# Self attention's last tile in two halves, a rebuilt end of a fixed convolution, and two mixtures that score their last tile apart: one change to a twelve-block network on one Trainium2 core

## The chip, the core and the metric

The kernel is one program on one core of a Trainium2 chip. The core has a matrix engine (TensorE; PE in the profile, with its weight loads as PEld), VectorE (DVE), ScalarE (ACT), GpSimd (POOL) and SyncE, which here only issues transfers (SP). Matrix products land in PSUM, which has eight banks of 128 partitions by 512 floats; everything else lies in SBUF or in the device's memory. The metric is the device time of one execution, in microseconds (us). Before the change the median of three runs is 3099.72 us (3099.47 to 3116.72).

## The reference

Sixteen sequences of 64 tokens with 256 channels, so 1024 tokens, go through four rounds of cross attention, a sequence mixer and a feed-forward block, each with a layer norm in front and added to the stream. Four of the twelve blocks matter here.

```python
x = x + L1_attn(_layernorm(x), ...)   # the fixed convolution
x = x + L1_ffn(_layernorm(x), ...)    # a mixture: 8 experts, 2 for each token
...
x = x + L3_attn(_layernorm(x), ...)   # self attention
x = x + L3_ffn(_layernorm(x), ...)    # a mixture with a capacity for each expert

# L1_attn
xz = rms_normed(x) @ in_proj_w.T + in_proj_b
x_ssm, gate = split(xz, 2)                       # 512 channels each
x_ssm = silu(conv_full(x_ssm, conv_w) + conv_b)  # 512 to 512 channels, 4 taps in time
ssm = conv_per_channel(x_ssm, K) + x_ssm * D     # K: 64 taps for each channel, fixed by weights
out = (ssm * silu(gate)) @ out_proj_w.T + out_proj_b      # and the block adds its own input

# L3_attn, 16 heads of 16 channels
scores = cov(q, k) + var(q) * var(k) / 16
out = (softmax(scores) @ v) @ Wo

# L1_ffn, L3_ffn
top_w, top_i = top_k(softmax(x @ gate_w), 2)
y = sum over the 2 chosen experts of  w * expert(x)
```

## The kernel before

The stream `X` stays in SBUF as eight tiles of 128 tokens (`NT` = 8). Products are in 32-bit floats, and each matmul of the program is two PE instructions in the profile; a transpose is one. A scheduler orders each engine's instructions at build time, by priority and its own estimate of when things are ready. Where the code says `set_order(True)`, instructions issued through `self.mm`, `self.tr` and the queues `dve`, `act` and `pool` keep the program's order on their engine.

**The fixed convolution** (`mamba_conv`, lines 1126 to 1260). The 512 channels are four groups `c` of 128; tokens go in two halves `n` of 512. `project(c, n)` (L1162) makes the input projection: groups 0 to 3 are the convolution's input, 4 to 7 become the gates `gs` through a Silu. `conv(c, n)` (L1183) is 16 matmuls of 512 columns, then a Silu into `xs[c]`. Groups 0, 1 and 2 then go through `taps` (L1196): VectorE adds 64 shifted products over the time steps, one instruction a tap. Group 3 goes through TensorE instead: `tokens` (L1212) transposes it, and `toeplitz(i, more)` (L1221) makes 32 channels by small matmuls against matrices read from the device's memory; between its pieces it puts the projections of the gates. `gated` multiplies the tap sums by the gates into `o`. All the order is written out: convolutions 0, 1, 2, 3, then tokens, four Toeplitz quarters, then the gating of all groups, and `out_proj` (L1262) does four matmuls for each tile (one for each group of `o`) and adds the tile to `X` (L1270). One PSUM pool, `mid`, has eight banks.

**The layer norm** (`layernorm`, L225) works on tiles 0 to 3, 4 to 6 and 7: VectorE takes means and variances, GpSimd the root (`rsqrt`), VectorE scales into `xn`. `norm_T` (L261) adds transposes of `xn` into `xnT`, by halves of four tiles.

**Self attention** (`attn3`, L1981) runs a pipeline over the eight tiles. For tile `i`: `scores` (32 matmuls for all 16 heads in two PSUM banks, then the row maximum and its subtraction on VectorE), `exps` on ScalarE, `probs_T` (transposes), `values` (matmuls against `v`, divided by the sum), `values_T`, `keep_T` and `output`, which adds to `X`. The steps of tile `i - 1` lie between those of tile `i`. The last round of the loop has only tile 7's values left.

**The mixtures** (`ffn1`, L2563, and `ffn3`, L2688) normalize and transpose, then `choose` (L2262) makes the eight gate logits of every token: 16 matmuls of 8 columns into one bank `pgate`, all after the last transpose. VectorE finds the two best experts. `slots` (L2344) gives each choice a place in its expert's list and inverts the lists by matmuls: `inb` marks the place within a group of 128 (VectorE, four pieces), `at` the group, and `val` holds three values to be moved (token row, weight, target row); `at` and `val` are made by GpSimd. The first inversion gives the rows that `take` gathers from the device's memory into `xg`; the other two (`pw`) give weights and targets. GpSimd also issues those gathers and the loads of expert weights (`up`, `down`). Then experts run, and `add_sent` (L2486) reads the two results of each token back (`yk`), GpSimd adds the two, and VectorE adds the sum to `X` (L2505), then a last product (L2509).

Of the kernel before, what the change touches and what calls it, by code (L numbers as in the profile page):

```python
# [8 lines left out]
F32 = mybir.dt.float32  # L9
# [69 lines left out]
class Net:  # L79
# [145 lines left out]
    def layernorm(self, dst, src, eps=1e-5, twice=None, then=None):  # L225

        nc = self.nc
        st = self.small.tile([P, NT, 6], F32, tag="st", name="st")
        mv = self.small.tile([P, NT, 2], F32, tag="mv", name="mv")
        rs = self.small.tile([P, NT], F32, tag="rstd", name="rstd")
        for lo, hi in ((0, 4), (4, 7), (7, 8)):
            for t in range(lo, hi):
                nc.vector.bn_stats(st[:, t, :], src[:, t, :])
                nc.vector.bn_aggr(mv[:, t, :], st[:, t, :])  # L238
            if twice is None:
                self.rsqrt(rs[:, lo:hi], mv[:, lo:hi, 1], 1.0, eps, hi - lo)  # L240
            else:
                self.rsqrt(rs[:, lo:hi], mv[:, lo:hi, 1], 1.0 + twice, eps * twice, hi - lo)
            for t in range(lo, hi):
                nc.vector.tensor_scalar(
                    dst[:, t, :], src[:, t, :], mv[:, t, 0:1], rs[:, t : t + 1], ALU.subtract, ALU.mult
                )
            if then is not None and hi % 4 == 0:
                then(hi // 4 - 1)
        return mv
# [876 lines left out]
    def mamba_conv(self):  # L1126
# [10 lines left out]
        with ExitStack() as es:  # L1137
            one = es.enter_context(tc.tile_pool(name=f"{L}one", bufs=1))
            two = es.enter_context(tc.tile_pool(name=f"{L}two", bufs=2))
            mid = es.enter_context(tc.tile_pool(name=f"{L}mid", bufs=8, space=PSUM))  # L1140
# [42 lines left out]
            def conv(c, n):  # L1183
                ps = mid.tile([P, 512], F32, tag="m", name="psc")
                for i in range(16):
                    ci, k = divmod(i, 4)
                    self.mm(
                        ps, wc[ci][:, k, c * P : (c + 1) * P], xp[:, ci, n * HB : (n + 1) * HB, k : k + TQ], i == 0, i == 15
                    )
                if n == 0:  # L1190
                    xs[c] = two.tile([P, B, TQ], F32, tag="xs", name="xs", bufs=4)
                act.activation(
                    xs[c][:, n * HB : (n + 1) * HB], ps.rearrange("p (b t) -> p b t", t=TQ), AF.Silu, bias=self.col(f"{L}_conv_b", c)
                )

# [25 lines left out]
            def toeplitz(i, more):  # L1221
# [5 lines left out]
                for d in range(TB):  # L1227
                    if d % (TB // 4) == 0:
                        next(more)
                    for r in (slice(0, 64), slice(64, 128)):  # L1230
                        self.mm(ps[r, d, :], T[r, d, :], xt[r, :, i * TB + d])
                act.copy(yt[:, :, i * TB : (i + 1) * TB], ps.rearrange("p d t -> p t d"))

# [7 lines left out]
            sums = [taps(0, 0, HB), taps(0, HB, B)]  # L1241
            for c in range(1, 4):
                for n in range(2):
                    conv(c, n)
                if c < 3:
                    sums.append(taps(c, 0, B))
            for g in range(2):
                tokens(g)
            for i in range(P // TB):
                toeplitz(i, (n for h in range(2) for n in project(4 + i, h)))  # L1250
            for x in sums:
                gated(*x)
            for g in range(2):
# [4 lines left out]
                dve.tensor_tensor(o[:, 3, cols], ps, gs[:, 3, cols], ALU.mult)  # L1258
            self.set_order(False)
            self.out_proj(o, wo, mid)  # L1260
# [720 lines left out]
    def attn3(self):  # L1981
# [11 lines left out]
        with ExitStack() as es:  # L1993
# [137 lines left out]

            project(0)
# [6 lines left out]
            for i in range(NT + 1):  # L2139
# [22 lines left out]
                if i + 2 < NT:  # L2162
                    keep(i + 2)
            self.set_order(False)
# [97 lines left out]
    def choose(self, wg, d_x, one, mid):  # L2262
# [13 lines left out]
        pg = mid.tile([P, 512], F32, tag="m", name="pgate")  # L2276

        nc.scalar.activation(best[:, 3, 0:1], self.xn[:, 0, 0:1], AF.Exp)

        def logits(g):  # L2280
            for t in range(4 * g, 4 * g + 4):
                for k in range(2):
# [6 lines left out]
                    )  # L2289

        for g in range(2):
            logits(g)
# [51 lines left out]
    def slots(self, place, oh, r, gate, comb, val, i, NG, one, big, mid, taken):  # L2344
# [7 lines left out]
        dve, act, pool = (  # L2352
            self.queue(n, e) for n, e in (("dve", nc.vector), ("act", nc.scalar), ("pool", nc.gpsimd))
# [11 lines left out]
        pool.tensor_tensor(at[:, :, :NG], at[:, :, :NG], at[:, :, 1:], ALU.subtract)  # L2365
        spot = self.spot.rearrange("p k t -> p (k t)")
        pool.tensor_tensor(val[:, 0, :, :NG], at[:, :, :NG], bc(spot, 2, NG), ALU.mult)
# [13 lines left out]
        for h in range(4):  # L2381
            js = slice(h * J // 4, (h + 1) * J // 4)
            dve.tensor_tensor(inb[:, js], bc(low[:, js], 2, P), bc(self.lane, 1, J // 4), ALU.is_equal)
        pi = mid.tile([P, 512], F32, tag="m", name="pi")
# [9 lines left out]
        pool.tensor_tensor(gate, gate, bc(r, 1, 2), ALU.mult)  # L2394
        pool.tensor_tensor(val[:, 1, :, :NG], at[:, :, :NG], bc(gate.rearrange("p k t -> p (k t)"), 2, NG), ALU.mult)
        pool.tensor_tensor(val[:, 2, :, :NG], at[:, :, :NG], bc(self.token, 2, NG), ALU.mult)
# [89 lines left out]
    def add_sent(self, d_y, sent, last, src, g, row, one, pool, mid):  # L2486
# [9 lines left out]
        for t in range(NT):  # L2496
# [4 lines left out]
            nc.gpsimd.tensor_tensor(yk[:, 0], yk[:, 0], yk[:, 1], ALU.add)  # L2501
            yks.append(yk)
        y = last()
        for t in range(NT):
            nc.vector.tensor_tensor(self.X[:, t, :], self.X[:, t, :], yks[t][:, 0], ALU.add)  # L2505
# [57 lines left out]
    def ffn1(self):  # L2563
# [6 lines left out]
        with ExitStack() as es:  # L2570
# [6 lines left out]
            self.norm_T(mid, "m")  # L2577
            p, oh, pq, seen, prod, gate = self.choose(wg, d_x, one, mid)
# [109 lines left out]
    def ffn3(self):  # L2688
# [4 lines left out]
        with ExitStack() as es:  # L2693
# [9 lines left out]
            self.norm_T(mid, "m")  # L2703
            p, oh, pq, _, prod, gate = self.choose(wg, d_x, one, mid)
# [170 lines left out]
```

## Time and profile before

The profiled execution took 3099.45 us, of which its span is 3097.8 us; 1.65 us lie around it. TensorE is busy for 94% of the span.

| engine | busy us | share of the span |
|---|---|---|
| PE | 2926.3 | 94% |
| DVE | 1962.2 | 63% |
| ACT | 1343.7 | 43% |
| POOL | 733.3 | 24% |

| stretch of the span (us) | what runs there |
|---|---|
| 1184 to 1368 | fixed convolution, its `out_proj` included |
| 1368 to 1378 | last transposes and logits of the first mixture |
| 1378 to 1407 | its choice and lists, up to the first expert |
| 1407 to 1601 | its experts and their sums |
| 2829 to 2934 | self attention |
| 2934 to 2943 | last transposes and logits of the second mixture |
| 2943 to 2966 | its choice and lists |
| 2966 to 3095 | its experts, sums and the results' adds |

A share of busy time over the whole span says little here: the change touches short stretches, and each is read by what ends last in it. In a timeline, columns are start, duration, engine, line, operation, output and inputs, shape and count; the square brackets give the idle time before and what ended it. In a table by windows, each engine's busy time in a stretch is followed by the clock that TensorE was granted (1.00 is full), the share of the transfer engines and their rate.

### The profile page before, as it was taken

Reading aid. Unit: us, or ns where it says so; the run is one execution under the profiler, and the core shown is the slowest. Engines: PE = TensorE matmul, PEld = TensorE weight load, DVE = VectorE, ACT = ScalarE, POOL = GpSimd, SP = SyncE. Lnnn points to the kernel's source line nnn. Section 1 sums busy time; section 2 is a strip of 40 time slices with the busy share of each in tenths; the row PEclk is TensorE's granted clock in tenths of the full one; section 3 lists DMA queues with packets and bytes.
Section 4 is the critical chain, followed back from the end, with each engine's and each line's share of the span. In section 5 each row is a group of like instructions: output and inputs, shape, how many; then the busy total and the mean of one; then the engine's idle time right before and its main releaser. Section 6 shows DMA issues by size and latency. Waiting matters only on the chain.

```text
span 3097.8 us, 65295 instructions
## 1 busy us (share of the span) xinstructions
PE 2926.3 (94%) x27452; PEld 1779.4 (57%) x27452; DVE 1962.2 (63%) x4058; ACT 1343.7 (43%) x3027; POOL 733.3 (24%) x817
## 2 busy tenths in 40 slices
PE   8999999899999999979989999998999899998888
PEld 4666666666455555458864555545655455455667
DVE  6888886523766665971137777768874676765521
ACT  3555554511554451013324444549851255554222
POOL 1000002400110001014420101026771355552132
PEclk9999999999999999979999999998998999999889
DMA  2000000013223323027752222101111111110143
GB/s 77 32 32 32 22 22 19 18 31 101 65 72 101 98 60 84 21 88 272 291 187 63 73 73 75 60 13 45 41 58 31 64 58 65 62 55 15 60 146 125
DMA packets 75820, 225.22 MB, mean 73 GB/s; under 512 B 17415, under 2 KB 30586, under 8 KB 68616
## 3 DMA queue, kind: packets, MB, share of 16 engines
q1 hardware_dynamic: 47536, 115.57, 12.1%
q0 software_dynamic: 21744, 99.34, 9.4%
q10 hardware_dynamic: 6248, 6.14, 0.7%
q8 instruction: 217, 3.56, 0.5%
q14 instruction: 75, 0.61, 0.1%
HBM read 210.09 MB, written 14.49 MB: 72 GB/s over the span
## 4 chain that ended last, share of the span: by engine, by line
PE 81%; DVE 12%; ACT 2%; POOL 2%; issue 2%; DMA 1%; SPq 0%; DVEq 0%; POOLq 0%; ACTq 0%
PE pss L205 15%; PE o L205 13%; PE pu L205 8%; PE pd L205 7%; PE psp L205 6%; PE pkv L205 5%; PE py L205 4%; PE pst L208 4%; PE po L205 2%; PE pb L208 2%; PE psq L205 2%; PE psy L205 1%; PE pg L205 1%; DVE nm L72 1%; PE ptk L208 1%
## 5 line engine op out<-in xcount | busy, mean ns | idle before, releaser
L205 PE MATMUL pss<-cT,qw 128*32 128x256 f32 x8192 | 368.3, 386 | 17.3 <-ACT pr L72 17.2
L72 DVE TENSOR_REDUCE nm<-pss 128x2 f32<-128x512 f32 (+1 forms) x384 | 309.4, 862 | 83.4 <-PE pss L205 83.4
L205 PE MATMUL o<-pT,cx 128*64 128x512 f32 (+3 forms) x1088 | 351.7, 576 | 0.0
L72 ACT ACTIVATE pr<-pss,nmm 128x256 f32<-128x256 f32 x512 | 234.8, 484 | 161.9 <-DVE nmm L72 161.9
L205 PEld LDWEIGHTS pss<-cT,qw 128*32 128x32 f32 x8192 | 203.6, 109 | 147.0 <-ACT pr L72 24.5
L222 POOL TENSOR_SCALAR rs<-mv 128x8 f32<-128x8 f32 (+3 forms) x50 | 9.7, 195 | 995.8 <-DVE mv L238 536.6
L205 PEld LDWEIGHTS o<-pT,cx 128*64 128x64 f32 (+1 forms) x1088 | 134.3, 163 | 188.4 <-issue 161.8
L72 ACT ACTIVATE pr<-pr,sm 128x256 f32<-128x256 f32 x256 | 109.1, 497 | 202.8 <-DVE sm L72 202.8
L205 PE MATMUL pkv<-wx,cT 128*128 128x512 f32 (+1 forms) x512 | 190.7, 625 | 0.6 <-issue 0.6
L72 DVE TENSOR_SCALAR pr<-pr,sm 128x256 f32<-128x256 f32 (+1 forms) x384 | 170.0, 485 | 6.6
L72 DVE TENSOR_TENSOR_SCAN h<-dA,pb 128x512 f32<-128x512 f32 x128 | 154.7, 1218 | 15.6 <-PE pb L208 9.3
L1512 POOL TENSOR_TENSOR h<-h,cb 128x1024 f32<-128x1024 f32 x64 | 151.5, 2369 | 53.2 <-DVE h L72 51.2
L205 PE MATMUL pd<-wd,hT 128*128 128x256 f32 x656 | 151.5, 382 | 2.6 <-DVE hT L2678 1.4
L72 DVE STREAM_TRANSPOSE pT<-pr 128x1024 f32<-128x1024 f32 x128 | 151.8, 1224 | 2.2
L2455 DVE TENSOR_SCALAR y<-pd,row 128x256 f32<-128x256 f32 x39 | 18.9, 484 | 207.5 <-PE pd L205 154.3
L72 ACT ACTIVATE pr<-pss,nm 128x1024 f32<-128x1024 f32 x128 | 142.7, 1115 | 11.2 <-DVE nm L72 8.6
L208 PE MATMUL pst<-ident,pr 128*128 128x128 f32 x1024 | 141.5, 281 | 5.8 <-DVE sm L72 1.9
L72 ACT COPY pT<-pst 128x512 f32<-128x512 f32 x128 | 75.0, 586 | 164.2 <-PE pst L208 164.2
L208 PEld LDWEIGHTS pst<-ident,pr 128*128 128x128 f32 x1024 | 110.5, 142 | 62.0 <-ACT pT L72 26.5
L205 PEld LDWEIGHTS pd<-wd,hT 128*128 128x128 f32 x656 | 122.0, 190 | 30.3 <-DVE hT L2678 6.2
L1686 POOL TENSOR_TENSOR rnk<-rnk,mhalf 128x8 f32<-128x8 f32 (+1 forms) x84 | 130.2, 1549 | 7.0
L205 PE MATMUL py<-h,ident 128*128 128x512 f32 x256 | 130.9, 597 | 0.0
(564 smaller groups left out, 5722.2 us busy)
## 6 DMA issues: line engine op xcount, KB each, us to landing
cT<-in_ctxT SPq DMA_DIRECT2D x32, 768.0 KB, 4.8
cx<-in_ctxP SPq DMA_DIRECT2D x32, 768.0 KB, 4.2
cT<-in_ctxT SPq DMA_DIRECT2D x32, 512.0 KB, 4.0
cT<-in_ctxT SPq DMA_DIRECT2D x64, 256.0 KB, 4.8
offb<-d_off SPq DMA_DIRECT2D x16, 576.0 KB, 3.8
cb<-d_C SPq DMA_DIRECT2D x16, 512.0 KB, 3.7
wu<-in_L_ffn_w POOLq DMA_DIRECT2D x8, 1024.0 KB
wd<-in_L_ffn_w POOLq DMA_DIRECT2D x8, 1024.0 KB
```

Of the source, the lines that this page charges most:

```text
L72: ins = getattr(self.engine, op)(*args, **kwargs)
L205: self.in_order(self.nc.tensor.matmul(out, lhsT=lhsT, rhs=rhs, start=start, stop=stop))
L208: self.in_order(self.nc.tensor.transpose(out, in_, self.ident))
L222: nc.gpsimd.tensor_scalar(t[:p, :n], in_, scale, eps, ALU.mult, ALU.add)
L1512: nc.gpsimd.tensor_tensor(hs[i], hs[i], cbs[hf, g], ALU.mult)
L1686: nc.gpsimd.tensor_tensor(r, r, self.mhalf[:, : n * H], ALU.pow)
L2455: nc.vector.tensor_scalar(y[:, i, :], po[:, i * D : (i + 1) * D], weight[:, g + i : g + i + 1], None, ALU.mult)
```

## The change

*Fixed convolution.* The PSUM banks are split: `mid` keeps four, and four (`held`) hold the out-projection's sums `pos` of all eight tiles, two to a bank. `conv` becomes a generator `convolved`, so that it can be cut into pieces of four matmuls. The order becomes: convolution 0, gates 4, convolutions 1 and 3, gates 5, tokens, then the first Toeplitz quarter with convolution 2 laid between its matmuls, and only then the taps of group 2. The other three quarters carry the projections of gates 7 and 6 and the out-projection's shares of groups 0 and 1. The shares of group 3, then 2, come at the end; `X` is added to in pairs of tiles.

*Self attention.* The loop ends one round and one tile earlier, and `last_tile(7)` does that tile by halves of heads.

*Mixtures.* `norm_T` goes; `choose` has `layernorm` call `normed` after each of its three groups of tiles, which transposes the group and makes its logits. `pgate` moves to the pool `big`. In `slots`, `at` and `val` go from GpSimd to VectorE. In `add_sent`, the odd tiles' two results are added to `X` by VectorE one after the other, with no sum by GpSimd.

```diff
-            mid = es.enter_context(tc.tile_pool(name=f"{L}mid", bufs=8, space=PSUM))
+            mid = es.enter_context(tc.tile_pool(name=f"{L}mid", bufs=4, space=PSUM))
+            held = es.enter_context(tc.tile_pool(name=f"{L}held", bufs=4, space=PSUM))
...
-            def toeplitz(i, more):
+            def toeplitz(i, more, every):
...
-                    if d % (TB // 4) == 0:
-                        next(more)
+                    if (i * TB + d) % every == 0:
+                        next(more, None)
...
+            def part(c, t):
+                first, last = t % 2 == 0 and c == 0, t % 2 == 1 and c == 2
+                self.mm(pos[t // 2][:, t % 2], o[:, c, t * P : (t + 1) * P], wo[:, c, :], first, last)
+
+            def rest():
+                for i in (7, 6):
+                    for h in range(2):
+                        yield from project(i, h)
+                for c in range(2):
+                    for t in range(0, NT, 2):
+                        part(c, t)
+                        part(c, t + 1)
+                        yield
...
             conv(0, 1)
-            sums = [taps(0, 0, HB), taps(0, HB, B)]
-            for c in range(1, 4):
+            projects(4, 0, 1)
+            for x in (taps(0, 0, HB), taps(0, HB, B)):
+                gated(*x)
+            for c in (1, 3):
                 for n in range(2):
                     conv(c, n)
-                if c < 3:
-                    sums.append(taps(c, 0, B))
+            projects(5, 0, 1)
+            gated(*taps(1, 0, B))
             for g in range(2):
                 tokens(g)
-            for i in range(P // TB):
-                toeplitz(i, (n for h in range(2) for n in project(4 + i, h)))
-            for x in sums:
-                gated(*x)
+            third = (n for h in range(2) for n in convolved(2, h))
+            toeplitz(0, third, 4)
+            for _ in third:
+                pass
+            third_sum = taps(2, 0, B)
+            more = rest()
+            for i in range(1, P // TB):
+                toeplitz(i, more, 6)
+            for _ in more:
+                pass
...
+            gated(*third_sum)
+            for c in (3, 2):
+                for t in range(NT):
+                    part(c, t)
+                    if c == 2 and t % 2:
+                        X = self.X[:, t - 1 : t + 1, :]
+                        nc.vector.tensor_tensor(X, X, pos[t // 2], ALU.add)
             self.set_order(False)
-            self.out_proj(o, wo, mid)
```

```diff
+            def last_tile(t):
...
+                halves = [slice(0, 4), slice(4, 8)]
+                for gs in halves:
+                    for g in range(gs.start, gs.stop):
+                        c, h = divmod(2 * g, 4)
+                        for b in range(2):
+                            for hh in range(2):
+                                r = slice(64 * hh, 64 * hh + 64)
+                                self.mm(ps[r, g, b, :], qb[:, c, b, h + hh, :], ka[:, c, b * TQ : (b + 1) * TQ])
+                    dve.tensor_reduce(mx[:, gs], ps[:, gs], AX.X, ALU.max)
+                    dve.tensor_tensor(pr[:, gs], ps[:, gs], bc(mx[:, gs], 3, TQ), ALU.subtract)
+                    act.activation(pr[:, gs], pr[:, gs], AF.Exp)
+                values(t - 1)
...
+                turned(0)
+                values_T(t - 1)
+                keep_T(t - 1)
+                turned(1)
+                for i in range(2):
...
+                            self.mm(o3[r, h - 8 * i, :], pT[r, h // 2, h % 2, :], v[r, h, :])
+                    dve.reciprocal(ri[:, hs], o3[:, :, HD])
+                    dve.tensor_tensor(on[:, hs], o3[:, :, :HD], bc(ri[:, hs], 2, HD), ALU.mult)
+                output(t - 1)
+                for i in range(2):
+                    pt = mid.tile([P, 512], F32, tag="m", name="pto")
+                    self.tr(pt[:, :P], on[:, 8 * i : 8 * i + 8].rearrange("p h d -> p (h d)"))
+                    (act.copy, dve.tensor_copy)[i](oT[:, i], pt[:, :P])
+                st[t]["oT"] = oT
+                output(t)
...
-            for i in range(NT + 1):
+            for i in range(NT - 1):
...
+            last_tile(NT - 1)
```

```diff
+        def normed(lo, hi):
+            if hi - lo == 1:
+                ps = mid.tile([P, 2, P], F32, tag="m", name="psT")
+                for c in range(2):
+                    nc.tensor.transpose(ps[:, c], self.xn[:, lo, c * P : (c + 1) * P], self.ident)
+                nc.vector.tensor_copy(self.xnT[:, :, lo * P : hi * P], ps)
...
+            for t in range(lo, hi):
                 for k in range(2):
                     nc.tensor.matmul(
                         pg[:, t * 8 : (t + 1) * 8],
...
+            if lo == 0:
+                nc.scalar.activation(best[:, 3, 0:1], self.xn[:, 0, 0:1], AF.Exp)
+
+        self.layernorm(self.xn, self.X, parts=normed)
...
-        pool.tensor_tensor(at[:, :, :NG], at[:, :, :NG], at[:, :, 1:], ALU.subtract)
-        pool.tensor_tensor(val[:, 0, :, :NG], at[:, :, :NG], bc(spot, 2, NG), ALU.mult)
...
             dve.tensor_tensor(inb[:, js], bc(low[:, js], 2, P), bc(self.lane, 1, J // 4), ALU.is_equal)
+            if h == 0:
+                dve.tensor_tensor(at[:, :, :NG], at[:, :, :NG], at[:, :, 1:], ALU.subtract)
+                dve.tensor_tensor(val[:, 0, :, :NG], at[:, :, :NG], bc(spot, 2, NG), ALU.mult)
...
-        pool.tensor_tensor(gate, gate, bc(r, 1, 2), ALU.mult)
-        pool.tensor_tensor(val[:, 1, :, :NG], at[:, :, :NG], bc(gate.rearrange("p k t -> p (k t)"), 2, NG), ALU.mult)
-        pool.tensor_tensor(val[:, 2, :, :NG], at[:, :, :NG], bc(self.token, 2, NG), ALU.mult)
+        dve.tensor_tensor(gate, gate, bc(r, 1, 2), ALU.mult)
+        dve.tensor_tensor(val[:, 1, :, :NG], at[:, :, :NG], bc(gate.rearrange("p k t -> p (k t)"), 2, NG), ALU.mult)
+        dve.tensor_tensor(val[:, 2, :, :NG], at[:, :, :NG], bc(self.token, 2, NG), ALU.mult)
...
-            nc.gpsimd.tensor_tensor(yk[:, 0], yk[:, 0], yk[:, 1], ALU.add)
+            if t % 2 == 0:
+                nc.gpsimd.tensor_tensor(yk[:, 0], yk[:, 0], yk[:, 1], ALU.add)
...
-            nc.vector.tensor_tensor(self.X[:, t, :], self.X[:, t, :], yks[t][:, 0], ALU.add)
+            for k in range(1 + t % 2):
+                nc.vector.tensor_tensor(self.X[:, t, :], self.X[:, t, :], yks[t][:, k], ALU.add)
```

## The prediction

> **What bounds the kernel now.** First the table by stage, since TensorE's 94% over the whole span hides stages with other limits. (Columns: busy time of PE, PEld, DVE, ACT, POOL, the clock granted, the transfers.)
>
> ```profile
> 1227.30:1309.60 82.30, 82.30 (x193) 35.88 (x193) 82.20 (x166) 4.13 (x6) 2.30 (x3) 1.00 0.05 12
> 1309.60:1347.20 37.60, 35.52 (x561) 22.51 (x559) 37.57 (x61) 8.74 (x15) 1.46 (x2) 0.99 0.11 32
> 1347.20:1378.30 31.10, 27.36 (x112) 23.73 (x112) 17.32 (x40) 2.66 (x4) 6.38 (x14) 0.72 0.36 117
> 1378.30:1406.90 28.60, 11.62 (x143) 8.79 (x143) 16.72 (x48) 2.29 (x4) 14.22 (x18) 0.54 0.68 263
> ```
>
> In the fixed convolution TensorE and VectorE are both full. Which ends last is in the chain of waits:
>
> ```profile
> 1260.86 0.66 DVE acc10e L72
> ...
> 1304.01 0.66 DVE acc20e L72
> ...
> 1347.16 0.61 DVE o L72
> 1347.82 10.10 PE po L205 x32
> ```
>
> It is VectorE: one group's taps take 1304.01 - 1260.86 = 43.15 us, they follow each other without a gap, and TensorE waits for the last. Then the timeline, for TensorE's pace and for what closes the other stages:
>
> ```profile
> 1213.39 96.35 PE L205 MATMUL psc<-xp,wc 128*128 128x512 f32 x224
> ...
> 1367.44 0.40 DVE L1270 TENSOR_TENSOR X<-X,po 128x256 f32<-128x256 f32 x1
> ...
> 1367.90 3.25 PE L268 MATMUL psT<-ident,xn 128*128 128x128 f32 x14 [3.08 <-DVE X L1270]
> ...
> 1371.86 6.41 PE L2283 MATMUL pgate<-wg,xnT 128*128 128x8 f32 x30
> ...
> 1405.97 0.41 PE L2439 MATMUL pxg<-ident,xg 128*128 128x128 f32 x2 [1.17 <-DMA xg<-L_ffnx,at]
> ...
> 2933.89 0.42 DVE L72 TENSOR_TENSOR X<-X,py 128x256 f32<-128x256 f32 x1 [2.17 <-PE py L205]
> ...
> 2959.96 4.08 PE L205 MATMUL pw<-inb,val 128*32 128x128 f32 x64 [2.96 <-POOL val L72]
> ```
>
> A mixture's transposes start when the last addition to X is done, though tiles 0 to 3 were normalized long before, and TensorE is then busy until the last logit. In the lists, the first mixture's first expert waits for gathered rows (a transfer), the second's later inversions for values that GpSimd makes.
>
> **Fixed convolution: a new wait.** An instruction pass of a 512-column matmul takes 96.35 / 224 = 0.430 us, so a half convolution is 32 x 0.430 = 13.76 us and a projection 1.72. From the end of convolution 0 (1213.39 + 13.76 = 1227.15) the new order on TensorE is: gates 4, 3.44; convolutions 1 and 3, 55.04; gates 5, 3.44; tokens, about 1.1 (to 1290.2); convolution 2's 27.52 with seven Toeplitz pieces before its last, each 0.52 and 0.20 of switching (a quarter in the timeline is 2.09 = 0.86 projection + 1.03 Toeplitz + 0.20). Convolution 2 ends at 1322.8 and its Silu (0.69, and 0.2 of hand-over) at 1323.7. In the old order it ended some 40 us earlier.
>
> VectorE meanwhile ends group 1's taps at 1260.86 + 1.2 (gating of group 0, moved ahead) + 43.15 = 1305.2 and its gating (1.14) at 1306.4, and its queue holds nothing else but group 2's taps. It idles 17.3 us. The last taps end at 1323.7 + 43.15 = 1366.9, **19.7 us later** than 1347.16. Queued behind them in VectorE's order: group 3's multiplication (0.65 a half), group 2's gating, the additions to X; TensorE waits with them. It runs out of Toeplitz work at 1290.2 + 33.3 + 29.3 + about 2 = 1354.8 (the three quarters: 12.4 Toeplitz, 6.9 projections, 6.9 for 16 early out-projection matmuls, 3.2 switching) and idles 13 us.
>
> What it buys: half of `out_proj` is done before. Let T be the end of the taps. Before, the last logit came at T + 31.1 (1378.27). After: the first late matmul runs at T + 0.8. TensorE restarted at 1347.8 after a wait of 1.9 us at clock 0.50 and had 1.00 only from about 1353.4. At 0.50 a 256-column matmul takes 0.85 us, then 0.43: in 5.6 us 6.6 of the 16, the rest 4.0, to T + 10.4. The Trainium skill ("TensorE: Matmul & The Clock Gate", Part 1: The HAM clock gate) has the clock back after one busy window of about 3.4 us; by that the matmuls would end 1.1 us sooner, and the whole 1.1 lower. VectorE, which took the statistics tile by tile in out_proj's shadow, now gets the pairs at T + 8 to T + 10.6, and owes four paired additions (0.68), eight statistics (0.62), eight scalings (0.36), two copies (1.1 together) and the last tile's root wait (1.3): 13 us, to T + 21. Last transposes, copy and four logit passes: 1.5; TensorE still has cold logits queued (0.2 a pass), about 1 more. I take T + 23.5; bounds T + 19 (the additions end at T + 11.3 and the second mixture's 8.3 us of transposes and logits follow at once) and T + 26 (nothing overlaps further). Gain 31.1 - 23.5 = 7.6. **Net +12.1** (+7.6 to +14.6). Four PSUM banks instead of eight: the third input projection may wait for the norm's last copies, 0.1; later turns of the four banks are 4 us or more apart with 0.7 us evictions, covered.
>
> **First mixture.** Scoring tile 7 apart is in the tail above; the table load for Exp (1.28) moves between ScalarE's two copies, hidden by queued logits, 1.3 if not. Lists: VectorE puts `at` and `val` (0.56 each by the 128x384 row) between pieces of `inb` (0.90 each), so the first inversion starts near 1390.9 instead of 1393.50, and rows come about 2 us earlier. But expert 0 waits for its gathered rows: `xg` was issued at 1397.96 and TensorE had it at 1405.97, behind five weight loads of 1 MB, running at 350 to 430 GB/s since 1390. Those start with `whose`, which is not moved. So -0.8 (less POOL work before loads 2 to 5). If the scheduler now fits a sixth load ahead of the rows, +2.7 (1 MB at 380 GB/s). I take +0.3, bounds -2.5 (one load less ahead) and +3.
>
> **Sums (both mixtures).** Four POOL additions fall (0.75 each); VectorE gets four more of 0.42, 20 in all, 8 us, about the time the reads take to land. The end stays VectorE's: -0.25 each, bounds -1 and +0.7. In the first mixture two of its eight additions of `yk` took 0.93 and 0.97, beside POOL's sums. A rule makes that speak against the change: the Trainium skill ("SBUF — State Buffer", Who interferes with whom) has a VectorE operation with two SBUF inputs and a GpSimd one that reads SBUF lock each other out. By it each of the four new additions could pay another 0.5: +2 a mixture instead.
>
> **Self attention.** From the scores' start (2916.41; unchanged until then) the old path is 17.9 us to the last addition's end, 2934.31. New: half the scores cold 1.84; maximum 0.65 and subtraction 0.65 for half 1 beside the second half's scores; half 2's end 2921.5, Exp 2922.2; tile 6's values on TensorE 2920.1 to 2922.1, transposes of half 1 to 2922.8, `values_T`, half 2's transposes to 2924.0, its copy 2924.8, value halves (1.0 each) to 2926.05, tile 6's output, two transposes and copies 2927.8, last output and addition 2929.5. **-4.8**; -3.3 if the clock falls on the way (the last four passes cold, +0.9, and transposes), -5.5 at best. The halved VectorE operations cost 0.1 more a pair (two of 0.67 against 1.23), in the count.
>
> **Second mixture.** Transposes and logits are TensorE's 7.82 busy of 8.40 us; apart or not, all 48 passes follow the last addition. Only the 0.5 gap goes: -0.4 (0 to -1.5 with a warm start). Its lists: `pw` ran at 2959.96, when GpSimd, between gathers, had made its values. On VectorE `at` and `val` (0.45 each) delay `inb` by 0.8, gate and the next two values end at 2957.0, then `pb` holds TensorE to 2957.8: `pw` 2.1 us earlier, with `xg` (issued about 0.8 later, 2.4 us to land) just there. -2.0 (-3 to +0.8, the last if the gather is late).
>
> Sum: 12.1 + 0.1 + 0.3 - 0.5 - 4.8 - 0.4 - 2.0 = **+4.8**. The profiled execution's 3099.45 gives 3104.25; the median of the runs shown is 0.27 above it, so 3104.5. Loads moved with these steps (gate weights' slots, the next block's weights on POOL) come free some us later and are used over 100 us on; cost nothing, or the 1 us issue if one lands in POOL's queue before a root.
>
> **Rivals.** (A) Not slower: the tail after the taps repays the wait. Place: from the last paired addition to the last logit. If VectorE keeps up, T + 19, 4.5 shorter: 3100.0; with the attention at its best 3099. It decides at T + 18.7. For it: warm, transposes cost 0.14 instead of 0.23. Against: 13 us of VectorE work behind pairs that come within 2.6 us. (B) The sixth load goes first in POOL's queue: +2.7 instead of +0.3, and the tail at T + 25: 3108.5. For it: two of POOL's operations that stood between the loads are gone. (C) The stall is not there, that is, group 2's convolution does not really come late: taps end at 1349.5, 17.3 less: 3087. Against: TensorE's order is written out, and the sum needs only rows.
>
> **How the numbers follow.** Forecast 0.50, A 0.20, B 0.22, C 0.04, other 0.04. So slower in any amount 0.74. Range 3095 to 3112: A with the good ends of lists, sums and attention (-5) below, B with the attention's and a list's bad ends (+3.5) above; that leaves out C, the rest and what lies beyond the bounds. A change of 1% (31 us), about what a measurement of this kernel can tell from none, no case reaches: 0.96 within, 0.01 faster, 0.03 slower, for a disturbance elsewhere in the schedule.
>
> **What would show it.** VectorE idle some 17 us before the third group's taps, ended by the Silu; TensorE idle 13 us before `part`, then at 0.50; last logit near 1390; `pxg` still waiting for `xg`; last attention addition 17.9 - 4.8 = 13.1 us after its scores start; `pw` waiting for no POOL row. No idle time before those taps would make the whole wrong; a tail under 19 us, its sign.

## The result, and the profile after

Over 17 runs of each kernel the median is 3115.54 us after the change (3110.28 to 3127.75) and 3108.94 us before (3099.44 to 3128.09). The ratio is 1.0008, with a 95% interval of 0.9992 to 1.0025: no change that can be told. (The two medians alone lie 6.6 us apart, which is within that interval.) As an absolute time the 3115.54 us lies above the forecast range of 3095 to 3112; but the kernel before, which the sum had started from at 3099.72, has moved up by 9.2 us as well, and the ratio applied to 3099.72 gives 3102.2. The two profiled executions are further apart, 3125.47 us (span 3123.8) after and 3099.45 before, because the one before is among the shortest of its kernel and the one after among the longest of its own. The 26.0 us between the two spans by stretch (worked out from the two traces):

| stretch | before | after | difference |
|---|---|---|---|
| start to the last addition ahead of the convolution | 1184.03 | 1180.37 | -3.7 |
| from there to the first use of the first mixture's logits | 194.28 | 210.90 | +16.6 |
| first mixture, to its last addition | 222.60 | 222.24 | -0.4 |
| unchanged code, to the scores of attention's last tile | 1315.51 | 1321.13 | +5.6 |
| last tile, to the last addition to X | 17.90 | 18.43 | +0.5 |
| from there to the first use of the second logits | 8.35 | 12.72 | +4.4 |
| rest | 155.09 | 157.99 | +2.9 |

Stretches of unchanged code move by -3.7 and +5.6, so a single profile can't price a change of this size. The table by windows of the changed kernel, with the windows at its own borders:

```profile
1226.10:1305.50 79.40, 79.40 (x249) 35.68 (x247) 79.19 (x163) 7.58 (x12) 0.00 (x0) 1.00 0.00 1
1305.50:1322.60 17.10, 17.10 (x114) 8.18 (x111) 0.06 (x2) 0.99 (x3) 2.76 (x4) 1.00 0.22 63
1322.60:1365.80 43.20, 30.59 (x434) 20.79 (x430) 43.17 (x66) 4.08 (x8) 0.99 (x2) 0.89 0.09 25
1365.80:1391.20 25.40, 19.20 (x80) 17.10 (x80) 12.54 (x35) 2.44 (x4) 6.34 (x14) 0.70 0.44 145
1391.20:1414.50 23.30, 12.55 (x136) 7.72 (x136) 17.16 (x50) 0.63 (x2) 10.18 (x12) 0.50 0.61 220
```

In the second line VectorE is busy for 0.06 of 17.10 us: the predicted stall. In the third TensorE has 30.59 us of work in 43.20, and nearly all of the rest is its 12.84 us wait for the last taps; the clock in the last two is low. The chain of waits of the changed kernel crosses the same places:

```profile
1318.19 3.65 PE psc L205 x8
1321.86 0.70 ACT xs L72
1322.58 0.79 DVE acc20e L72
...
1365.77 0.69 DVE o L72
1366.51 6.32 PE po L205 x20
1372.92 0.70 DVE X L1300
```

Before, it was VectorE from tap to tap without a break; now the end of convolution 2 sets the start of the last taps. The timeline of the changed kernel:

```profile
1202.04 5.37 PE L205 MATMUL psc<-xp,wc 128*128 128x512 f32 x8 [2.58 <-DMA wc<-in_L_attn_conv_wT]
...
1322.58 0.79 DVE L72 TENSOR_SCALAR acc20e<-xs,taps 128x1024 f32<-128x1024 f32 x1 [17.04 <-ACT xs L72]
...
1366.51 8.90 PE L205 MATMUL po<-wo,o 128*128 128x256 f32 x32 [12.84 <-DVE o L72]
...
1414.55 0.66 PE L2548 MATMUL pxg<-ident,xg 128*128 128x128 f32 x2 [0.51 <-DMA xg<-L_ffnx,at]
...
2938.14 1.15 PE L205 MATMUL pss<-ka,qb 128*64 128x64 f32 x32 [1.52 <-DVE pr L72]
...
2952.65 0.42 DVE L72 TENSOR_TENSOR X<-X,py 128x256 f32<-128x256 f32 x1 [1.38 <-PE py L205]
...
2952.99 2.68 DVE L244 TENSOR_SCALAR xn<-X,mv,rstd 128x256 f32<-128x256 f32 x3
...
2980.04 4.33 PE L205 MATMUL pw<-inb,val 128*32 128x128 f32 x61
```

The waits of 17.04 and 12.84 us are those that were forecast. `pxg` still waits for `xg` and `pw` for no row of GpSimd, as forecast too. Three lines were not forecast: the convolution waits 2.58 us for its fourth weight load; in attention the second half of the scores waits for VectorE's subtraction of the first half; three scalings of the norm behind attention take 2.68 us, where one takes 0.41.

### The profile page after: what moved, and what is told of

Its sections match the earlier page's. It is cut to its first block, busy times and chain, and to the rows that moved or that the text cites. A ratio compares the mean times of both kernels' runs of the same rounds, so it can differ in the third digit from the quotient of the medians.

```text
span 3123.8 us, 65282 instructions
## 1 busy us (share of the span) xinstructions
PE 2943.9 (94%) x27452; PEld 1787.5 (57%) x27452; DVE 1965.6 (63%) x4078; ACT 1343.8 (43%) x3029; POOL 721.2 (23%) x799
## 4 chain that ended last, share of the span: by engine, by line
PE 85%; DVE 9%; ACT 2%; DMA 1%; POOL 1%; issue 1%; SPq 0%; DVEq 0%; POOLq 0%; ACTq 0%
PE pss L205 15%; PE o L205 13%; PE pu L205 8%; PE pd L205 7%; PE psp L205 6%; PE pkv L205 5%; PE py L205 4%; PE pst L208 4%; PE psc L205 3%; PE po L205 2%; PE pb L208 2%; PE psq L205 2%; PE psy L205 1%; PE pg L205 1%; PE ptp L208 1%
## 5 line engine op out<-in xcount | busy, mean ns | idle before, releaser
L208 PEld LDWEIGHTS pst<-ident,pr 128*128 128x128 f32 x1024 | 109.8, 141 | 61.5 <-ACT pT L72 26.5
L205 PEld LDWEIGHTS pkv<-wx,cT 128*128 128x128 f32 (+1 forms) x512 | 64.3, 188 | 118.6 <-issue 92.2
```

Source lines behind the costliest of these rows:

```text
L205: self.in_order(self.nc.tensor.matmul(out, lhsT=lhsT, rhs=rhs, start=start, stop=stop))
L208: self.in_order(self.nc.tensor.transpose(out, in_, self.ident))
```

## The experiments

Twelve kernels ran. Stretches are named as in the table above; "T" is the end of the third group's taps, as in the prediction.

**One part at a time.** Three kernels take the kernel before and only the change's edits to `mamba_conv`, to `attn3`, or to the mixtures.

> The kernel before with the fixed convolution's new end alone; attention and mixtures as before. My theory: convolution 2 comes too late, so VectorE idles about 17 us ahead of the third group's taps, the taps end 18 to 20 us later than in the kernel before, and the shorter tail behind them returns 5 to 8 us: the stage from the last addition before it to the first use of the logits is 11 to 17 us longer, the run 11 to 17 us (0.35 to 0.55%) above the kernel before. Rival (clock): most of the 26 us between the two profiles is where cold stretches of TensorE's clock happened to fall; then the wait is there but the run lies within 5 us of the kernel before, and the stage is not over 8 us longer.

Measured: the stretch took 211.27 us, 17.0 more, with the stall (17.03 us), and T + 22.8 to the first use of the logits. Yet the median was 3107.95 us against 3113.05, ratio 0.9989 (0.9971 to 1.0006). So the profile went as my theory said and the time as the rival's. The profiled execution (3116.4) was one of the two longest of the twelve. A stretch that is 17 us longer with a run that is not suggests that the old end, in most executions, costs more than the first profile shows; the experiments below look for that.

> The kernel before with the halves of heads in self attention's last tile alone. My theory: the second half's scores wait 1.5 us for VectorE's subtraction of the first half, since both halves are one PSUM tile, and what the halves should have hidden is lost: 17 to 19 us from the start of the tile's scores to the last addition (17.9 before), and the run within 3 us of the kernel before. Rival (clock): the 18.4 us of the changed kernel came from a cold clock, and here it is 13 to 15.5 us, the run 2 to 5 us lower.

Measured: 20.0 us, worse than either theory, and 12.16 us instead of 8.35 from there to the logits, with code there that is unchanged; the clock was 0.50 for 58 us on end. The 1.52 us wait for VectorE is there as in the changed kernel. Median 3118.61, ratio 1.0019 (0.9998 to 1.0040): a loss of 6 us at the middle of the interval, though zero lies just within it.

> The kernel before with the mixtures' changes alone (last tile scored apart, values by VectorE, half of the sums by VectorE). My theory: in the second mixture VectorE's copies stand ahead of the last tile's statistics, so the stretch from the last addition to the first use of the logits is 10 to 12 us instead of 8.35; the first mixture's stretch from there to its first gathered rows at TensorE is 3 to 4.5 us shorter (27.7 before), but its experts take it back; in all the run is within 4 us of the kernel before. Rival (clock): the 12.7 us in the changed kernel is the cold clock alone, here 8 to 9 us, and the run is 3 to 6 us lower than the kernel before.

Measured: 10.27 us; first gathered rows at 23.02 us instead of 27.66; ratio 0.9991 (0.9966 to 1.0015). The time is the one forecast, but not its cause: VectorE did the last tile's statistics at once here. This profile holds the convolution of the kernel before, and shows what that first profile didn't. The timeline in the Toeplitz quarters, two lines of the kernel before first, then this one's:

```profile
1317.17 1.13 PE L205 MATMUL psi<-xnT,w_in 128*128 128x512 f32 x2
1318.22 1.10 PE L205 MATMUL psT<-xt,T 64*64 64x8 f32 x32
...
1346.94 2.07 PE L205 MATMUL psi<-xnT,w_in 128*128 128x512 f32 x2
...
1348.95 1.88 PE L205 MATMUL psT<-xt,T 64*64 64x8 f32 x32
...
1364.50 14.53 PE L205 MATMUL po<-wo,o 128*128 128x256 f32 x64
```

The clock had fallen at 1324.7 for 41 us. A projection of two passes took 2.07 us instead of 1.13, a piece of 32 small products 1.88 instead of 1.10; the quarters took 49.4 us instead of 32.4 and ended 14 us behind T, and the last addition of the out-projection came 34.0 us after T instead of 20.7.

**The late convolution undone.**

```diff
-            for c in (1, 3):
+            for c in (1, 2, 3):
...
-            third = (n for h in range(2) for n in convolved(2, h))
-            toeplitz(0, third, 4)
...
-            for i in range(1, P // TB):
-                toeplitz(i, more, 6)
+            for i in range(P // TB):
+                toeplitz(i, more, 8)
```

> As the kernel with the convolution's new end alone, but convolution 2 back between 1 and 3, all four Toeplitz quarters carrying the gates 7 and 6 and the early products. My theory: VectorE does not wait for the third taps (under 1 us), they end within 4 us of the kernel before's, TensorE ends its Toeplitz work at about the same time, the tail is about 25 us as in the changed kernel, and the run is 14 to 20 us lower than with the new end alone and 2 to 7 us lower than the kernel before. Rival (PSUM banks and order: the new end is slow for its four banks and its paired additions, not for the late convolution): the run is within 5 us of the kernel with the new end alone.

Measured: ratio 0.9989 (0.9967 to 1.0012). It tested nothing, because VectorE now waited 12.1 us for group 1's gates, whose projection had come to stand behind three convolutions. Mended by putting `projects(5, 0, 1)` behind convolution 1:

> The convolution's new end alone, with convolutions in the order 0, 1, 2, 3 and the gates 5 between 1 and 2, so that VectorE finds both the third group's input and group 1's gates ready; Toeplitz quarters with a dense piece after every 8 channels, as in the kernel before. My theory now has two parts: (a) the late convolution costs VectorE 15 to 19 us; (b) the small Toeplitz products let TensorE's clock fall in part of the executions, and the old end (a dense piece every 8 channels) pays some 12 us for it there. By it: no wait ahead of the third taps (under 1 us), they end at 1347 to 1353, 16 to 20 us sooner than in the kernel with the new end alone when the stage starts alike; the runs spread over 15 us or more, as the kernel before's do, the fastest below 3094, the median 3098 to 3106. Rival (the wait is free, since the tail takes it back): median within 3 us of the new end alone, 3105 to 3111.

Measured: no wait ahead of the third taps, T 140.7 us after the first tap (157.7 with the late convolution). Still the median was 3111.88, ratio 1.0008 (0.9985 to 1.0032), the runs from 3095.47 to 3121.72. In its profile the clock fell at 1345.4, in the middle of the quarters, without a wait:

```profile
1343.12 1.13 PE L205 MATMUL po<-wo,o 128*128 128x256 f32 x4
1344.18 1.10 PE L205 MATMUL psT<-xt,T 64*64 64x8 f32 x32
1345.22 1.95 PE L205 MATMUL po<-wo,o 128*128 128x256 f32 x4
1347.10 1.88 PE L205 MATMUL psT<-xt,T 64*64 64x8 f32 x32
```

The taps end 17.0 us sooner after the first tap than with the new end alone, and the first use of the logits comes at T + 35.4 instead of T + 22.8. So 17 us less stall bought nothing that the runs can tell: part (a) holds in the trace, and in this profile 12.6 us of it go where part (b) says.

**More dense pieces between the small products.** The gates 4 and 5 go into the quarters too.

```diff
-                for i in (7, 6):
+                for i in (4, 5, 7, 6):
...
             for i in range(P // TB):
-                toeplitz(i, more, 8)
+                toeplitz(i, more, 5)
+                if i == 1:
+                    for x in sums:
+                        gated(*x)
+                    third_sum = next(third)
```

> As the kernel named last, but the gates 4 and 5 also lie within the Toeplitz quarters, with a dense piece after every 5 channels (24 pieces instead of 16), and VectorE multiplies by the gates in the middle of the third taps. By part (b) of my theory the clock stays at 1.00 through the Toeplitz quarters in nearly all executions: the runs spread over 12 us or less, mean clock 0.962 or more, median 3092 to 3101 and at least 3 us below the kernel with a piece every 8 channels. Rival (the density of the pieces has nothing to do with the clock): same spread and median within 2 us of that kernel, or slower by the 2 us of switching more.

Measured: median 3102.05, runs from 3097.94 to 3106.32, mean clocks 0.963 to 0.967, ratio 0.9980 (0.9962 to 0.9999). The spread is a third of the other's, and all is as forecast but the median, 1 us above its range. The table by windows of this kernel, first the quarters, then the end:

```profile
1317.20:1354.00 36.80, 36.80 (x476) 22.66 (x477) 36.73 (x60) 6.61 (x11) 0.70 (x1) 1.00 0.08 25
1354.00:1382.90 28.90, 22.94 (x168) 19.20 (x166) 12.41 (x34) 2.92 (x5) 5.99 (x14) 0.81 0.39 128
```

Up to T TensorE is busy throughout at a clock of 1.00. Over all profiles: with a piece every 8 channels the clock fell in the midst of the quarters in 5 of 7, with one every 6 or 5 in none of 6, though in the four with one every 5 it came down within 0.7 us of the quarters' last product.

**No pieces at all.** The kernel before, gates first, then the quarters alone:

```diff
             for i in range(P // TB):
-                toeplitz(i, (n for h in range(2) for n in project(4 + i, h)))
+                projects(4 + i, 0, 1)
+            for i in range(P // TB):
+                toeplitz(i, iter(range(4)))
```

> The kernel before, the same work, but the gates' projections all ahead of the Toeplitz quarters, so that nothing dense lies between their small products. My theory (the small products let TensorE's clock fall, the dense pieces between them decide how often): it falls in nearly all executions; in the profile the clock is 0.50 over most of the last two quarters and the first use of the logits comes 38 us or more after the third taps' end (31.1 and 28.9 in the warm profiles of the old end, 41.3 in the cold one); no run under 3105, median 3113 to 3124. Rival (it is only the phase of the clock's windows, whatever lies between): spread, fastest runs (near 3096) and median as the kernel before's, within 3 us.

Measured: median 3101.47, ratio 0.9965 (0.9947 to 0.9984). My theory was right on the clock of the profile and wrong on its price. The table by windows, gates, quarters, end:

```profile
1317.80:1331.60 13.80, 13.80 (x34) 5.89 (x32) 13.80 (x15) 5.39 (x8) 0.00 (x0) 1.00 0.15 38
1331.60:1357.10 25.50, 25.50 (x513) 25.38 (x512) 25.46 (x48) 1.80 (x4) 0.70 (x1) 0.55 0.08 23
1357.10:1387.40 30.30, 26.16 (x121) 23.70 (x120) 14.46 (x37) 3.03 (x5) 6.24 (x14) 0.78 0.36 117
```

The quarters ran at 0.55, as predicted, but the 13.80 us of projections ran ahead of them at 1.00, and T + 33.5 is all it comes to. In the kernel before, a fall also halves the speed of every projection that lies between the quarters' products. An estimate from these rows: the small products alone would take 16 pieces of 1.03 us (from start to start, in the kernel before), 16.5 us, at full clock and took 25.5, so about 9 of the 17 us that the quarters lost in the profile above are theirs, and the other 8 the dense work's among them.

**Two PSUM tiles in attention.**

```diff
-                ps = ps_s.tile([P, 8, 2, TQ], F32, tag="s", name="pss")
+                pss = [pool.tile([P, 4, 2, TQ], F32, tag=tag, name="pss") for pool, tag in ((ps_s, "s"), (mid, "m"))]
...
-                for gs in halves:
+                for ps, gs in zip(pss, halves):
```

> Attention's last tile by halves alone, with the two halves' scores in two PSUM tiles instead of one. My theory: TensorE no longer waits 1.5 us for VectorE's subtraction between the halves; from the tile's first score to the last addition 15.5 to 18 us (20.0 with one tile), the run 2 to 6 us below the kernel with one tile and within 3 us of the kernel before. Rival (the wait is not what costs, the clock after the halves' small pieces is): the wait is gone, but the stretch is still 18.5 us or more, and the stretch behind it, to the logits, still 11 to 13 us.

Measured: 12.49 us, less than forecast; the wait is gone. From there to the logits 12.59 instead of 8.35, so 25.1 together, against 26.3 before: of 5.4 us saved, 4.2 went in the next stretch. Ratio 1.0011 (0.9990 to 1.0033); the profiled execution is the shortest of the ten. The timeline:

```profile
2912.10 3.68 PE L205 MATMUL pss<-ka,qb 128*64 128x64 f32 x64
...
2925.01 1.98 DVE L244 TENSOR_SCALAR xn<-X,mv,rstd 128x256 f32<-128x256 f32 x3 [0.43 <-POOL rstd L223]
...
2927.51 0.41 DVE L237 BATCH_NORM_STATS2 st<-X 128x6 f32<-128x256 f32 x1
...
2930.24 0.69 PE L268 MATMUL psT<-ident,xn 128*128 128x128 f32 x2 [2.21 <-DVE xn L244]
```

The last tile's statistics come 2.9 us after its addition (2924.16 + 0.42), behind scalings and a copy of other tiles.

**The last tile's statistics ahead.** In the mixtures alone, tiles 4 to 6 are handed to `normed` only when the last tile is scaled:

```diff
-            if parts is not None:
-                parts(lo, hi)
+            if parts is not None and hi != 7:
+                if hi == 8:
+                    parts(4, 7)
+                parts(lo, hi)
```

> The mixtures' changes alone, but tiles 4 to 6 are transposed and scored only after the last tile is scaled, so that VectorE does the last tile's statistics ahead of the copies of the others. My theory: in the second mixture the stretch from the last addition to the first use of the logits is 8 to 9.3 us (10.3 with the mixtures' changes as they are, 8.35 in the kernel before). Rival (TensorE's clock and order set it, not VectorE's order): 10 us or more.

Measured, in one execution: 10.32 us; my theory fell. What this profile shares with that of the mixtures alone is GpSimd's queue: a weight load (`wd`, 0.95 us to issue) stands between the two steps of the last root, which ends 3.6 us after the statistics instead of 2.6, and the logits behind it run at a clock of 0.50. That this makes up the difference is argued from the rows; no run took the load away.

**Put together.** Three kernels carry the dense pieces and the mixtures' changes, with the last products by pairs of tiles. The first keeps attention as before:

```diff
-            for c in (3, 2):
-                for t in range(NT):
+            for p in range(NT // 2):
+                for c, t in ((2, 2 * p), (2, 2 * p + 1), (3, 2 * p), (3, 2 * p + 1)):
                     part(c, t)
```

> The kernel with a dense piece every 5 channels, plus the mixtures' changes, attention as before; the last products go by pairs of tiles (group 2, then 3), and the last tile's statistics stand ahead of the copies. My theory: the savings add, since they lie in different stages: median 3094 to 3101, ratio 0.995 to 0.998, clock 0.963 or more. Rival (what a stage saves is lost in the next, as the first mixture's lists did with 4.6 us): within 2 us of the kernel with the dense pieces alone, or above it.

Measured: median 3101.68, ratio 0.9974 (0.9955 to 0.9994). By the median it is the rival, 0.4 us below the kernel with the dense pieces; the ratio lies in the theory's range too. The mixtures' changes add nothing that can be told. The second also has the two PSUM tiles, and VectorE's order held to the last statistics first:

```diff
-                nc.vector.bn_stats(st[:, t, :], src[:, t, :])
-                nc.vector.bn_aggr(mv[:, t, :], st[:, t, :])
+                dve.bn_stats(st[:, t, :], src[:, t, :])
+                dve.bn_aggr(mv[:, t, :], st[:, t, :])
...
+            if parts is not None and hi == 7:
+                roots(7, 8)
```

> As the kernel named last, but with attention's last tile by halves in two PSUM tiles, and VectorE held to the last tile's statistics ahead of the scaling of tiles 4 to 6. My theory: the halves save 5 us up to the last addition, and with the statistics first the norm behind does not give them back: from the last tile's scores to the first use of the logits 19 to 23 us (26.3 in the kernel before, 25.1 with two PSUM tiles alone), the run 2 to 6 us below the kernel named last. Rival (the clock that falls in the halves' small pieces takes it): 24 us or more, the run within 2 us of the kernel named last.

Measured: median 3102.87, ratio 0.9978 (0.9958 to 0.9997); 24.1 us from the scores to the logits. The rival's number, but not for its reason: the clock was 1.00 through the halves, which took 10.84 us, and fell only at 2938.1, behind them. Its timeline:

```profile
2935.97 0.30 POOL L2605 MEMSET zero<- 128x256 f32 x1
...
2936.21 2.55 DVE L72 TENSOR_SCALAR xn<-X,mv,rstd 128x256 f32<-128x256 f32 x1
...
2937.70 0.73 POOL L2462 MEMSET val<- 128x768 f32 x1
...
2938.69 0.19 POOL L222 TENSOR_SCALAR rs<-mv 128x1 f32<-128x1 f32 x1
```

One scaling took 2.55 us, as long as GpSimd wrote its constants, and the last root stood behind these. The third moves these constants behind the root:

```diff
         self.layernorm(self.xn, self.X, parts=normed)
+        const = constants()
...
+    def after_root(self, ins):
+        order = mybir.DependencyInfo(mybir.DependencyClass.NoSync, mybir.DependencyReason.DATA)
+        self.tc.add_manual_dep(ins.ins, self.last_root.ins.name, order, reason="after the norm")
```

> As the kernel named last (halves in two PSUM tiles, statistics first), but GpSimd's constants of the two mixtures stand behind the last tile's root in its queue. My theory: in that kernel VectorE's first scaling behind attention took 2.55 us instead of 0.41, because GpSimd was writing these constants from SBUF's side at the same time, and the last root stood behind them; with the constants behind the root all scalings take 0.32 to 0.55 us, and from the last addition to the first use of the logits it is 8.5 to 11 us (13.3 there); from the last tile's scores to there 19.5 to 22.5 us (24.1 there, 26.3 in the kernel before); the run 1 to 4 us below it. Rival (that scaling was long for another reason, and the cold clock sets the logits' time): a scaling of over 1 us is still there, or the stretch is 12 us or more; the run within 1.5 us of it.

Measured: 9.87 us to the logits, 22.4 in all, scalings of 0.40 to 0.81 us; median 3098.47 against 3112.35, ratio 0.9961 (0.9944 to 0.9978).

```profile
2930.73 0.96 POOL L186 DMA_DIRECT2D wd<-in_L_ffn_w  x1
2930.96 0.81 DVE L72 TENSOR_SCALAR xn<-X,mv,rstd 128x256 f32<-128x256 f32 x1
2931.77 0.18 POOL L226 TENSOR_SCALAR rs<-mv 128x1 f32<-128x1 f32 x1
```

In the trace the theory holds, but for one scaling of 0.81 us beside the issue of a load by GpSimd. Of the run, the stretch explains 1.8 us; the medians differ by 4.4, but the two were measured apart, and the intervals of their ratios to the kernel before overlap. This kernel has the lowest median of all, 0.2 to 0.6% below the kernel before.

## Why the prediction was right, and where it was not

The class was right, and so was the stall, the larger part of the largest term. The sum of +4.8 us lies in the interval of the runs (-2.5 to +7.8, from the ratio), but by luck: two of its terms, what the old end costs and what attention saves, are wrong by more than the sum.

- *The stall.* 17.3 us forecast, 17.04 measured; the taps end 19.7 us later by the forecast, 157.68 - 138.01 = 19.67 from the first tap; TensorE's wait 13 against 12.84. A written-out order and a row's duration are enough for this.
- *The tail*, T + 23.5 forecast, T + 25.4 and T + 22.8 measured: mis-sized by 2 at most, within its bounds. The late products restarted at 1366.51 and had the clock back at 1370.0, 3.5 us later, where I had taken 5.6. The Trainium skill ("TensorE: Matmul & The Clock Gate", Part 1: The HAM clock gate) says one busy window of about 3.4 us, free-running; the three rows (3.5, 4.1 in the convolution alone, 5.6 before) fit such a window met at different points.
- *The entry*, 0.1 for four PSUM banks: missed. In the eight profiles with the new end TensorE reaches the convolution 8.6 us after the last addition instead of 10.5, finds the fourth weight load not there, waits 2.3 to 5.0 us (none to 2.0 with the old end), and goes on at a clock of 0.50: the first tap comes 27.5 to 31.1 us after the last addition in eight profiles, against 25.1 to 27.3 in six with the old end. Why it gets there sooner was not tested.
- *"Before, the last logit came at T + 31.1"*: the step that failed. It rests on one value of a quantity that varies: from T to the out-projection's last addition it was 20.7, 21.7, 23.3, 34.0 and 37.2 us in five profiles of that same old end. The prediction knew only the fall at TensorE's 1.9 us wait (which, in the trace, came at 1346.6, 0.7 us into that wait); the fall within the Toeplitz quarters it never considered. With a piece every 6 or 5 channels no profile shows it. Over the 108 runs of the kernel before that were taken beside the experiments, 29 have a mean clock of 0.963 or more and a median of 3098.3 us, 79 less and 3114.1. The profile and two of the three first runs belonged to the rarer kind. A line through these runs gives 2.75 us more for each 0.001 less of mean clock, with 1.8 us left over; the convolution alone lies 11 us above that line and 0.0041 higher in clock, which is 11 us as well. So by this line, which is a fit and not an experiment, the +12.1 is about right at a given clock, and the clock takes it back.
- *Attention*, -4.8: wrong. The step "maximum 0.65 and subtraction 0.65 for half 1 beside the second half's scores" doesn't happen, since both halves are one PSUM tile and the second write waits for the first read. With two tiles the stretch is 12.5 (forecast 13.1), so the other steps together were right. But 4.2 us went back in the norm behind: the last tile's statistics now stood 2.9 us behind its addition, after three scalings beside GpSimd's constants (0.66 each instead of 0.41) and a copy. Statistics ahead alone did not help (13.3 us to the logits); with the constants moved too it was 9.87.
- *First mixture's lists*, +0.3: the rows came 4.4 us sooner, since they are asked for behind three weight loads instead of five. The first expert's product came 2.1 us sooner (26.5 us after the logits instead of 28.6), and the stage as a whole gained about 2.0 (219.6 on average in six profiles with the change, 221.5 in eight without). What holds the first expert up for the rest was not tested.
- *Second mixture*: logits -0.4 forecast. With the mixtures alone it was +1.9, and there "the 1 us issue if one lands in POOL's queue before a root" did land. In the changed kernel it was +4.4, with the last tile's statistics 3.6 us behind its addition. Lists -2.0 forecast, -0.2 measured: `pw` ran 3.0 us sooner, but the first expert started 4.1 us behind the gathered rows instead of 2.1. In one profile of the same lists (the last tile's statistics ahead) they took 19.5 instead of 23.2. What held the result of `pw` in the other profiles stays open.
- *Sums*, -0.25 each: +0.3 in the second mixture, from its last expert product to the end (11.49 and 11.75), within the bounds.

Not settled: how much of the change's time each part holds. The three parts alone come to -3.4, +5.9 and -2.8 us, each with an interval of some 5 to 8 us to either side.

## What to carry to other kernels

Before a profile is used as the base of a sum, look at where its execution lies among the runs, and at the clock of each stage: a stage in which the clock falls in some executions and not in others has two lengths. Dense work put between small products here either kept the clock up or was slowed with them, so mix it tightly or keep it apart. When a stage ends earlier, look at what the next one now runs beside: here constants on GpSimd that had always been out of the way.

## What was not expected of the hardware

- TensorE's clock falls while it is never idle: 25.5 us of products of 8 columns, busy throughout, at a mean clock of 0.55. In the five other profiles in which it fell within the quarters, too, TensorE shows no gap there before the fall. Mixing in dense pieces more often kept it up; what exactly sets it, no run here shows.
- A second write to a PSUM tile waited for a read of its other half, in another bank; two tiles removed the 1.52 us. So the wait came from the program's ordering by tiles.
- VectorE's scaling of 128x256 took 2.55 us beside GpSimd's constants, 0.41 alone. The Trainium skill ("SBUF — State Buffer", Who interferes with whom) says that `tensor_scalar` can take both ports and then excludes GpSimd or is blocked by it for a whole instruction, which agrees in kind; here the 2.55 us cover a row of GpSimd's writes, the longest of 0.98 us, and not one of them. The prediction had used that section only for additions.
